# Layer 0's scaled blocks added by one VectorE reduce a tile, all form additions on GpSimd, form sets for all seven outer terms

## The chip, the core and the metric

The kernel runs on one core of a Trainium2 chip. TensorE (PE) multiplies matrices into PSUM; VectorE (DVE), ScalarE (ACT) and GpSimd (POOL) work on tiles in SBUF, and the first two also read PSUM; SyncE (SP) here only issues DMA transfers. Each engine takes its instructions in one stream, and a stream waits on counters (semaphores) that other engines and transfers raise. The metric is the device time in microseconds (us); lower is better. All numbers are float32.

## The reference

Input: x of shape (B=8, N=2048, F=64), a dense row-normalised adjacency A of 2048 x 2048, and small weights. Four layers follow each other, each `x = layernorm(x + layer(x))`:

```python
# layer 0: Chebyshev supports [I, A, 2 A A - I], weights made per node from an embedding with D = 16
w = einsum('nd,dkio->nkio', embedding, weight);  b = einsum('nd,do->no', embedding, bias)
out = einsum('bnki,nkio->bno', einsum('knm,bmc->bnkc', A_stack, x), w) + b
# layer 1: twice  z = relu((A @ z) @ W_i)
# layer 2: x @ W_self + (A @ x) @ W_neighbor + bias
# layer 3: concat(x, A x, 2 A A x - x, A x, 2 A A x - x) @ W + bias
```

What costs time is the product of the 2048 x 2048 matrix A with a 2048 x 512 block (all batches and features side by side), which is needed seven times, and layer 0's product with per-node weights: for each node the 64 features of three supports are multiplied with 16 matrices, and the 16 results are added with the node's 16 embedding values as factors.

## The kernel before

**Products with A.** The first product is made while A comes in, slice by slice, and on the way VectorE stores sums of blocks of A ("comb") in DRAM. The other six are calls of `product`, counted here as products one (layer 0's second) to six, each a fast scheme at two levels; four and six add their result in place. At the outer level A is taken as 2 x 2 blocks of 1024, and seven "outer terms" (A11, S1, A12, S2, S4, S3, A22 in order of time) are multiplied. Within a term there are two recipes:

- `inner`: a scheme of seven products of 512 x 512 blocks. `mul` loads 1 MB into a ring of buffers "a", seven of its eight chunks in all, and issues four matmuls of 512 columns (or 16 of 128 when the result is added in place into xy, `onto_slot`); the PSUM tiles are mma, mmb, mmc. A matmul in float32 shows as two records in the profile.
- `fast_inner`: 26 smaller products in 13 pairs (`PAIRS`), each with an operand from a "set of forms" of that term (26 blocks of 256 KB that lie in DRAM) and with one from x, made on GpSimd by seven additions of 512 values a partition and four of 256 (f, d, fn, fm). It has 52 matmuls of 256 columns, or 104 of 128 in place; the PSUM tiles are mm.

A set of forms is made once, by the generator `make_forms`, from four 1 MB tiles of the term: four raw blocks are stored as they are (`RAW`), and the list `SUMS` names 28 additions or subtractions of 128 x 512; 22 of the results are stored, one DMA each, issued by SP (L270). Those named in `POOLED` (ten) are GpSimd's, the other eighteen VectorE's (L290, L293). Four terms (`FORMED`) have sets: S1's is made in layer 0's product, those of A12, S2 and S4 at the start of the second.

**Layer 0's feature step.** `product(1, feature0)` hands each finished quarter block to `feature0(g, p, hT)`: 16 groups, each of four node tiles of 128 for one pair of batches. For each tile, TensorE multiplies the three supports (x, A x, A A x, as the tiles xT, tT and C) with the weights wn into two PSUM tiles y, eight matrices each (L1519; four y buffers). VectorE scales and adds the first eight blocks onto xy (L1529, one scalar_tensor_tensor each, with the node's embedding value as the factor); ScalarE scales the other eight into the SBUF tile s (L1533), and GpSimd adds those up in halves, 512, 256 and 128 values, and then onto xy (L1539, L1542). `fetch` (L1498) loads xT and tT of the next group through SP, into two buffers each.

**Order.** `Pump` runs the feature steps between terms. In layer 0 they are held back: four groups run after term S2, twelve at the start of the second product, and beside them the forms' generator is stepped (`Pump.run` with `side` and `rate`). After it the second product's seven terms follow. The instructions under `keep_in_program_order` stay in the order in which they are written on their engine; others are placed by a scheduler when the program is built. Each engine, SP too, then executes its own fixed order. SP's order holds the loads of A and of forms (L249, L252, L254), the stores of forms (L270) and the fetches (L1498).

## Time and profile before

| | us |
|---|---|
| median of 3 runs | 1649.23 (1647.22 to 1649.6) |
| profiled execution, its own time | 1647.88 |
| its span | 1646.0 |
| layer 0's feature step, first run (four groups) | from 306.6 |
| layer 0's feature step, second run (twelve groups) | 464.0 to 711.8 |
| second product's first matmul | 715.0 |

| engine | busy us | share of the span |
|---|---|---|
| TensorE, matmul | 1623.3 | 99% |
| TensorE, weight loads (beside the matmuls) | 1154.6 | 70% |
| VectorE | 1122.0 | 68% |
| ScalarE | 308.7 | 19% |
| GpSimd | 574.5 | 35% |

The profile shows one execution. For each group of instructions it gives how often it ran, its busy time and the mean of one; for idle time it names what ended it. The chain of work that ended last is followed back from the last instruction: what stands in it set the time. A name like `y<-wn,xT` is an output tile and its inputs; L1519 is line 1519 of the kernel.

### The profile page before, as it was taken

The numbers are of one execution on the slowest core, as the hardware profiler recorded it, in microseconds if no ns is written. First come the engines' busy times: TensorE is split into PE (matmuls) and PEld (weight loads), VectorE is DVE, ScalarE is ACT, GpSimd is POOL, SyncE is SP. The second block draws the span as 40 slices with busy tenths as digits, with TensorE's granted clock in tenths as the row PEclk, the third lists the DMA queues.
The fourth block names the chain that finished last, engine by engine and source line by source line (L and its number), as shares of the span: only waits on it lengthen the run. The fifth ranks groups of instructions, "written<-read, shape, count | busy, mean of one in ns | idle before, by whom it ended". The sixth has DMA issues, their size and how long they took to land.

```text
span 1646.0 us, 23252 instructions
## 1 busy us (share of the span) xinstructions
PE 1623.3 (99%) x8886; PEld 1154.6 (70%) x8886; DVE 1122.0 (68%) x1889; ACT 308.7 (19%) x870; POOL 574.5 (35%) x582
## 2 busy tenths in 40 slices
PE   9999999999999999999999999999999999999998
PEld 5998944444444444438865787589999788669998
DVE  5996885686458878846753477974688556644687
ACT  0210100143024444421111111221111112100111
POOL 1121100284037778764502350034512441025510
PEclk9999999999999999999999999999999999999999
DMA  8999999746853645278777776566888866677885
GB/s 315 358 389 370 334 342 326 250 141 237 307 178 123 203 141 187 101 310 312 277 287 262 288 280 253 208 227 234 295 293 301 292 234 213 237 255 282 310 307 175
DMA packets 101390, 429.47 MB, mean 261 GB/s; under 512 B 10752, under 2 KB 31616, under 8 KB 61856
## 3 DMA queue, kind: packets, MB, share of 16 engines
q1 hardware_dynamic: 87616, 380.34, 64.8%
q0 software_dynamic: 12016, 46.27, 7.5%
q8 instruction: 71, 1.16, 0.3%
q10 hardware_dynamic: 1648, 1.38, 0.3%
q14 instruction: 39, 0.32, 0.1%
HBM read 346.16 MB, written 81.79 MB: 260 GB/s over the span
## 4 chain that ended last, share of the span: by engine, by line
PE 94%; DVE 3%; DMA 1%; issue 1%; POOL 0%; ACT 0%; ACTq 0%; SPq 0%; DVEq 0%; POOLq 0%
PE y L1519 19%; PE mm L443 15%; PE mm L437 10%; PE mmb L565 10%; PE mmc L565 7%; PE mma L565 7%; PE ps_n L1301 6%; PE mmb L558 4%; PE ps_i L1215 3%; PE z L1573 3%; PE mmc L558 2%; PE mma L558 2%; PE z L1602 2%; PE ps_n L1255 1%; PE pt L1564 1%
## 5 line engine op out<-in xcount | busy, mean ns | idle before, releaser
L1539 POOL TENSOR_TENSOR s<-s 128x512 f32<-128x512 f32 (+2 forms) x192 | 166.2, 865 | 254.3 <-ACT s L1533 244.1
L1529 DVE SCALAR_TENSOR_TENSOR xy<-y,e_sb,xy 128x128 f32<-128x128 f32 x512 | 179.4, 350 | 65.3 <-PE y L1519 49.4
L1533 ACT ACTIVATE s<-y,e_sb 128x128 f32<-128x128 f32 x512 | 139.3, 383 | 196.2 <-PE y L1519 178.3
L565 PE MATMUL mmb<-a,t 128*128 128x512 f32 x360 | 161.9, 592 | 0.0
L443 PE MATMUL mm<-a,f 128*128 128x256 f32 x576 | 135.1, 380 | 1.1 <-POOL f L389 1.0
L1519 PE MATMUL y<-wn,xT 64*128 64x512 f32 x512 | 131.4, 590 | 0.0
L1519 PE MATMUL y<-wn,C 64*128 64x512 f32 x512 | 131.2, 589 | 0.0
L1519 PE MATMUL y<-wn,tT 64*128 64x512 f32 x512 | 131.1, 589 | 0.0
L389 POOL TENSOR_TENSOR f<-T 128x512 f32<-128x512 f32 x20 | 26.5, 1340 | 276.7 <-PE mmb L565 124.7
L565 PEld LDWEIGHTS mmb<-a,t 128*128 128x128 f32 x360 | 67.3, 190 | 79.4 <-issue 78.7
L443 PEld LDWEIGHTS mm<-a,f 128*128 128x128 f32 x576 | 108.7, 190 | 17.7 <-POOL f L389 1.9
L437 PE MATMUL mm<-f,a 128*128 128x128 f32 x768 | 92.4, 275 | 0.0
L1519 PEld LDWEIGHTS y<-wn,xT 64*128 64x128 f32 x512 | 49.5, 187 | 60.9 <-issue 57.3
L1519 PEld LDWEIGHTS y<-wn,tT 64*128 64x128 f32 x512 | 49.6, 187 | 60.2 <-issue 59.7
L1519 PEld LDWEIGHTS y<-wn,C 64*128 64x128 f32 x512 | 49.5, 187 | 60.4 <-issue 60.4
L437 PEld LDWEIGHTS mm<-f,a 128*128 128x128 f32 x768 | 89.0, 192 | 0.1
L476 DVE TENSOR_TENSOR p<-p,mm 128x512 f32<-128x512 f32 x60 | 41.0, 684 | 61.3 <-PE mm L443 41.7
L319 DVE TENSOR_TENSOR u<-mmb,p 128x512 f32<-128x512 f32 x44 | 30.2, 686 | 67.5 <-PE mmb L565 58.1
L466 DVE TENSOR_TENSOR C<-C,mm 128x512 f32<-128x512 f32 x80 | 54.2, 684 | 29.3 <-PE mm L443 22.3
L565 PE MATMUL mma<-a,T 128*128 128x512 f32 x160 | 72.1, 593 | 0.0
L1023 POOL DMA_DIRECT2D comb<-si x29 | 22.0, 758 | 137.8 <-DVE si L1014 137.8
L558 PE MATMUL mmb<-t,a 128*128 128x128 f32 x576 | 67.3, 275 | 0.0
(243 smaller groups left out, 3024.7 us busy)
## 6 DMA issues: line engine op xcount, KB each, us to landing
a<-comb SPq DMA_DIRECT2D x127, 1024.0 KB, 5.0
a<-form SPq DMA_DIRECT2D x120, 1024.0 KB, 4.8
a<-in_blocks SPq DMA_DIRECT2D x43, 1024.0 KB, 4.9
comb<-si POOLq DMA_DIRECT2D x29, 1024.0 KB, 10.6
form<-form SPq DMA_DIRECT2D x88, 256.0 KB, 2.8
a<-in_slices SPq DMA_DIRECT2D x15, 1024.0 KB, 10.9
comb<-so POOLq DMA_DIRECT2D x15, 1024.0 KB, 12.8
a<-form SPq DMA_DIRECT2D x20, 512.0 KB, 4.8
```

Of the source, the lines that this page charges most:

```text
L437: nc.tensor.matmul(ps[:, ts(2 * h + j, P)], a[:, j, m, :], x[:, m, :], start=(start and h == j == m == 0), stop=(m == 1), skip_group_check ...
L443: nc.tensor.matmul(ps[:, ts(h, GW // 2)], x[:, m, :], a[:, :, m, :], start=(start and h == m == 0), stop=(m == 1), skip_group_check=True,)
L466: nc.vector.tensor_tensor(out, out, view(v), op)
L558: nc.tensor.matmul(to, a[:, k, m, :], xb[:, m, :], start=(start and opens and m == 0), stop=(m == TG - 1), skip_group_check=True,)
L565: nc.tensor.matmul(ps, xb[:, m, :], a[:, :, m, :], start=(start and m == 0), stop=(m == TG - 1), skip_group_check=True,)
L1215: nc.tensor.matmul(ps, x[:, m // 2, m % 2], s[n](m), start=(start and m == 0), stop=(m == TG - 1), skip_group_check=True,)
L1301: nc.tensor.matmul(ps[:, ts(p, GW // 2)], b(k, p), a(k // TG, k % TG), start=(start and p == k == 0), stop=(k == NT // 2 - 1), skip_group_ ...
L1519: mm = nc.tensor.matmul(y[:, b, :], terms[n][half, ts(k, P)], wn[half, n, h * DH : (h + 1) * DH, :], start=(n == 0), stop=(n == 2),)
L1529: tc.keep_in_program_order(nc.vector.scalar_tensor_tensor(acc, y[:, :, ts(d, F)], e, acc, ALU.mult, ALU.add))
L1533: nc.scalar.activation(s[:, d], y[:, :, ts(d, F)], AF.Copy, scale=e)
L1539: nc.gpsimd.tensor_tensor(s[:, :n], s[:, :n], s[:, n : 2 * n], ALU.add)
L1573: nc.tensor.matmul(z[:, k, :], aT[:, ts(k, P)], wd[:, w, :], start=(n == 0), stop=(n == len(terms) - 1),)
```

## The change

Three things change together.

1. **Layer 0's tile.** VectorE's scalar_tensor_tensor now takes six of the sixteen blocks (`DIRECT = 6`), and the sixth writes its sum to slot 0 of a larger tile s. ScalarE scales the other ten into slots 1 to 10. One VectorE tensor_reduce adds the eleven slots into xy. It is issued by `settle` after the next tile's six additions, or when `Pump.run` ends. GpSimd has no part in it any more.
2. **The forms' additions.** All 28 additions of a set are GpSimd's; two negations a set ("n", "m"), by ScalarE, take the place of the three-operand form that VectorE had. `SUMS` is reordered. When a tile of a set has been read for the last time, the next set's tiles are loaded (`COMING`); the third and fourth tile lie in buffers "T" where several sets are made in a row.
3. **Seven sets instead of four.** Layer 0's product makes S3's set beside its first four groups and uses it. The second product makes six sets (S1, A12, S2, S4, A22, A11) beside its twelve groups, at 2.02 steps of the generator for each step of the features (1.08 before), and uses all but A11's itself. Products three to five form all seven terms; the last forms all but A22.

The descriptor scratch of the DMAs that GpSimd issues is halved (`dynamic_dma_scratch_size`).

```diff
@@ -22,7 +22,7 @@
 
 A11, A12, A22, S1, S2, S3, S4 = range(7)
 A21 = 7
-FORMED = (S1, A12, S2, S4)
+FORMED = (S1, A12, S2, S4, S3, A22, A11)
 
 
 
@@ -37,17 +37,17 @@
 ROWS = ((0, 0), (1, 0), (0, 1), (1, 1))
 RAW = {11: (2, 2), 14: (1, 1), 19: (0, 2), 23: (1, 0)}
 SUMS = (
-    (16, (0, 1), (0, 3), 1), (5, (2, 0), (2, 3), 1), ("d", (2, 1), (2, 2), 1), ("c", (0, 0), (0, 2), 1),
-    (6, 16, (1, 3), 0), (18, 6, "d", 1), (21, (1, 1), "d", 1), (4, 21, (1, 2), 1),
-    (1, (1, 3), (2, 3), 1), (2, 1, (2, 0), 1), (15, 2, "c", -1), (0, "c", (1, 0), 0),
-    (20, (1, 2), 0, -1), (10, (3, 1), (3, 2), 1), ("f", 10, (3, 3), 1), (17, "f", 1, -1),
-    (7, (0, 1), 10, -1), ("b", (0, 0), (1, 0), 1), (12, (0, 3), (1, 3), 1), (24, (3, 0), (3, 2), 1),
-    (3, (2, 0), 24, -1), ("a", (1, 1), (2, 1), 1), (8, (3, 0), (2, 0), -1), (22, (3, 1), (0, 1), -1),
-    (9, 7, "b", -1), ("e", 24, (3, 3), 1), (13, "e", 12, -1), (25, 3, "a", -1),
+    (5, (2, 0), (2, 3), 1), ("n", (0, 0), None, None), ("c", "n", (0, 2), -1), (0, "c", (1, 0), -1),
+    (20, (1, 2), 0, -1), (1, (1, 3), (2, 3), 1), (2, 1, (2, 0), 1), (15, 2, "c", 1), (10, (3, 1), (3, 2), 1),
+    ("f", 10, (3, 3), 1), (17, "f", 1, -1), (7, (0, 1), 10, -1), ("b", (0, 0), (1, 0), 1), (9, 7, "b", -1),
+    (16, (0, 1), (0, 3), 1), ("d", (2, 1), (2, 2), 1), ("m", (1, 3), None, None), (6, "m", 16, -1),
+    (18, 6, "d", 1), (21, (1, 1), "d", 1), (4, 21, (1, 2), 1), (24, (3, 0), (3, 2), 1), (3, (2, 0), 24, -1),
+    ("a", (1, 1), (2, 1), 1), (25, 3, "a", -1), (8, (3, 0), (2, 0), -1), (22, (3, 1), (0, 1), -1),
+    (12, (0, 3), (1, 3), 1), ("e", 24, (3, 3), 1), (13, "e", 12, -1),
 )
 HALF = {13: 0, 22: 0, 8: 1, 17: 1}
-POOLED = {5, 18, 4, 15, 20, 17, 12, 22, 9, 25}
-SPENT = 24
+COMING = (8, 12, 16, 26)
+DIRECT = 6
 
 
 def unit(i, j):
@@ -61,6 +61,7 @@
     def __init__(self):
         self.jobs = []
         self.later = []
+        self.ended = None
         self.rate = 1
         self.gate = None
         self.owed = 0
@@ -114,6 +115,8 @@
                         side.pop(0)
             self.jobs.pop(0)
             n = None if n is None else n - 1
+        if self.ended is not None:
+            self.ended()
         for job in side:
             for _ in job:
                 pass
@@ -171,7 +174,6 @@
     DH = D // 2
     RING = 4
     TB = 9
-    LANDING = 4
     BLK = TG * GW
 
     big = ctx.enter_context(tc.tile_pool(name="big", bufs=1))
@@ -237,12 +239,15 @@
     pieces = []
     p_mm = p_y = None
 
-    def load(q, s, forms=False):
+    def load(q, s, forms=False, home=None):
         nonlocal loads
-        loads += 1
-        turn = loads % (RING + 3)
-        pool = ring2 if ring2 is not None and turn >= RING else ring
-        a = pool.tile([P, TG, TG, P], F32, tag="a", name="a")
+        if home is None:
+            loads += 1
+            turn = loads % (RING + 3)
+            pool = ring2 if ring2 is not None and turn >= RING else ring
+            a = pool.tile([P, TG, TG, P], F32, tag="a", name="a")
+        else:
+            a = home
         flat = a.rearrange("p n m c -> p (n m c)")
         if forms:
             size = min(4, len(SLOT) - 4 * s) * GW
@@ -259,7 +264,7 @@
             tc.keep_in_program_order(pieces.pop(0)())
         return a
 
-    def make_forms(*qs):
+    def make_forms(*qs, landing):
 
 
         pin = tc.keep_in_program_order
@@ -269,8 +274,13 @@
             dst = formed[q][k // 4][:, ts(k % 4, GW)]
             nc.sync.dma_start(dst.rearrange("p (n m c) -> p n m c", n=2, m=2), f)
 
-        coming = [load(qs[0], s) for s in range(4)]
-        for _ in range(LANDING):
+        def fetch(q, s):
+            return load(q, s, home=None if len(qs) == 1 or s < 2 else sums.tile(
+                [P, NT // 2, 4 * F], F32, tag="T", name="T", bufs=3
+            ).rearrange("p t c -> p (t c)").rearrange("p (n m c) -> p n m c", n=TG, m=TG))
+
+        coming = [fetch(qs[0], s) for s in range(4)]
+        for _ in range(landing):
             yield
         for i, q in enumerate(qs):
             tiles, coming, made, done = coming, [], {}, []
@@ -286,23 +296,20 @@
                 store(q, n, raw(*ik))
             for k, (n, a, b, sign) in enumerate(SUMS):
                 f = sums.tile([P, 2, 2, P], F32, tag="t", name="form", bufs=TB)
-                if sign == 0:
-                    pin(nc.vector.scalar_tensor_tensor(f, source(a), -1.0, source(b), ALU.mult, ALU.subtract))
-                else:
-                    eng = nc.gpsimd if n in POOLED else nc.vector
-                    pin(eng.tensor_tensor(f, source(a), source(b), ALU.add if sign > 0 else ALU.subtract))
                 made[n] = f
+                if sign is None:
+                    nc.scalar.activation(f, source(a), AF.Copy, scale=-1.0)
+                    continue
+                pin(nc.gpsimd.tensor_tensor(f, source(a), source(b), ALU.add if sign > 0 else ALU.subtract))
                 if not isinstance(n, str):
-                    done.append((q, n, f))
+                    done.append((n, f))
                 yield
                 while len(done) > 1:
-                    store(*done.pop(0))
-                if k > SPENT and len(coming) < 2 and i + 1 < len(qs):
-                    coming.append(load(qs[i + 1], len(coming)))
+                    store(q, *done.pop(0))
+                while i + 1 < len(qs) and len(coming) < 4 and k >= COMING[len(coming)]:
+                    coming.append(fetch(qs[i + 1], len(coming)))
             for job in done:
-                store(*job)
-            while len(coming) < 4 and i + 1 < len(qs):
-                coming.append(load(qs[i + 1], len(coming)))
+                store(q, *job)
 
     def product(src, feature, between=None, rate=1, own=None, pin=False, runs=None, onto_slot=None, ends=False, fast=(), forms={}):
 
@@ -707,10 +714,10 @@
                 yield
 
         def side(q, b=None):
-            return [make_forms(*forms[q]), prepare_sums(b)] if q in forms else []
+            return [make_forms(*forms[q], landing=8 if waits else 5), prepare_sums(b)] if q in forms else []
 
         if waits:
-            pump.run(None, side(A11, b11), 1.08)
+            pump.run(None, side(A11, b11), 2.02)
             pump.hold = False
         pump.pass_mark()
 
@@ -1497,6 +1504,17 @@
                     for tile_, src in zip(fetched[i, p], (xT, t1T)):
                         pin(nc.sync.dma_start(tile_, src[p][:, ts(i, GW)]))
 
+            open_sums = []
+
+            def settle():
+                while open_sums:
+                    acc, s = open_sums.pop(0)
+                    tc.keep_in_program_order(
+                        nc.vector.tensor_reduce(acc, s.rearrange("p d b f -> p b f d"), AX.X, ALU.add)
+                    )
+
+            pump.ended = settle
+
             def feature0(g, p, hT):
                 if (g, p) == order[0]:
 
@@ -1510,7 +1528,7 @@
                     acc = xy[:, 0, t, ts(p, 2 * F)].rearrange("p (b f) -> p b f", f=F)
 
 
-                    s = l0y.tile([P, DH, 2, F], F32, tag="s", name="s", bufs=2)
+                    s = l0y.tile([P, D - DIRECT + 1, 2, F], F32, tag="s", name="s", bufs=2)
                     for h in range(2):
                         y = p_y.tile([P, 2, DH * F], F32, tag="y", name="y")
                         for n in range(3):
@@ -1525,26 +1543,23 @@
                                     tc.keep_in_program_order(mm)
                         for d in range(DH):
                             e = e_sb[:, t, h * DH + d : h * DH + d + 1]
-                            if h == 0:
+                            if h == 0 and d < DIRECT:
                                 tc.keep_in_program_order(nc.vector.scalar_tensor_tensor(
-                                    acc, y[:, :, ts(d, F)], e, acc, ALU.mult, ALU.add
+                                    s[:, 0] if d == DIRECT - 1 else acc, y[:, :, ts(d, F)], e, acc, ALU.mult, ALU.add
                                 ))
                             else:
-                                nc.scalar.activation(s[:, d], y[:, :, ts(d, F)], AF.Copy, scale=e)
+                                nc.scalar.activation(
+                                    s[:, 1 + h * DH + d - DIRECT], y[:, :, ts(d, F)], AF.Copy, scale=e
+                                )
                         if h == 0:
+                            settle()
                             yield
-                    n = DH // 2
-                    while n:
-                        tc.keep_in_program_order(
-                            nc.gpsimd.tensor_tensor(s[:, :n], s[:, :n], s[:, n : 2 * n], ALU.add)
-                        )
-                        n //= 2
-                    tc.keep_in_program_order(nc.gpsimd.tensor_tensor(acc, acc, s[:, 0], ALU.add))
+                    open_sums.append((acc, s))
                     yield
 
 
             RUNS = {A12: 1, S2: NP}
-            product(1, then(feature0, 0, gap=4), lambda: pump.add(sum_wn()), rate=4, runs=RUNS, forms={S2: (S1,)})
+            product(1, then(feature0, 0, gap=4), lambda: pump.add(sum_wn()), rate=4, runs=RUNS, forms={S2: (S3,)}, fast=(S3,))
 
 
     late = p_z = None
@@ -1586,7 +1601,7 @@
         nc.vector.scalar_tensor_tensor(part(g, p, 0), z, 0.0, part(g, p, 0), ALU.max, ALU.add)
         yield
 
-    product(0, feature1a, to_late, pin=True, fast=FORMED, forms={A11: (A12, S2, S4)})
+    product(0, feature1a, to_late, pin=True, fast=FORMED[:6], forms={A11: (S1, A12, S2, S4, A22, A11)})
     def both_terms(src, w, b):
 
         def own(g, p):
@@ -1659,7 +1674,7 @@
         ("w_l3", np.asarray(L3_gnn_weight)),
         ("b_l3", np.asarray(L3_gnn_bias).reshape(1, F)),
     ]
-    nc = bacc.Bacc("TRN2", target_bir_lowering=False, num_devices=1, dynamic_dma_scratch_size=8192)
+    nc = bacc.Bacc("TRN2", target_bir_lowering=False, num_devices=1, dynamic_dma_scratch_size=4096)
     arrays, args = {}, []
     for name, a in layout:
         a = np.ascontiguousarray(a)
```

## The prediction

> **What bounds the kernel now.** I read the page's busy table first, then the chain that ended last, then stages of it by window, and last the waits of the queues that the change touches. A "set" below is the forms of one outer term (28 GpSimd adds after the change); a "group" is one run of layer 0's feature step, four node tiles.
>
> ```profile
> span 1646.0 us, 23252 instructions
> PE 1623.3 (99%) x8886; PEld 1154.6 (70%) x8886; DVE 1122.0 (68%) x1889; ACT 308.7 (19%) x870; POOL 574.5 (35%) x582
> ...
> PE 94%; DVE 3%; DMA 1%; issue 1%; POOL 0%; ACT 0%; ACTq 0%; SPq 0%; DVEq 0%; POOLq 0%
> PE y L1519 19%; PE mm L443 15%; PE mm L437 10%; PE mmb L565 10%; PE mmc L565 7%; PE mma L565 7%; PE ps_n L1301 6%; PE mmb L558 4%; PE ps_i L1215 3%; PE z L1573 3%; PE mmc L558 2%; PE mma L558 2%; PE z L1602 2%; PE ps_n L1255 1%; PE pt L1564 1%
> ```
>
> TensorE is busy 99% of the span and is 94% of the chain; the next stretch of the chain is always another matmul. So only two things can move the time: fewer matmul columns, or a wait that TensorE does not have now.
>
> ```profile
> core 0: us, PE busy (x) PEld busy (x) DVE busy (x) ACT busy (x) POOL busy (x), PEclk, DMA share, GB/s
> ...
> 464.00:711.80 247.80, 247.42 (x1153) 111.44 (x1152) 195.70 (x467) 108.06 (x386) 187.05 (x218) 1.00 0.45 147
> ```
>
> This window is the second and longer stretch of layer 0's projection (the "main run": 12 groups, 48 tiles, the y matmuls). The columns are busy times by engine; TensorE has no gap: 247.8/48 = 5.16 us a tile, 20.6 a group. VectorE and GpSimd have room (196 and 187 of 248), so neither limits it.
>
> ```profile
> 464.02 239.70 PE y L1519 x1116
> 708.25 6.65 DMA a<-in_blocks
> 715.03 5.29 PE mma L565 x8
> ...
> 801.40 34.54 PE mm L443 x160
> ...
> 1483.62 3.57 PE mmc L558 x32
> ...
> 1494.34 69.69 PE mm L437 x624
> ```
>
> Start, length, work. Here are the prices of a term by both recipes: a plain inner product is 7 products of 3.43 us (3.57 when it adds in place), a formed one is 52 matmuls of 256 columns or 104 of 128. 160 records in 34.54 us are 0.216 each, and a formed term has 104 such records: 22.5 against 24.0 us. In place, 624 records in 69.69 us are three terms of 23.2 against 25.0. The 6.65 us of DMA at 708.25 is the one place where TensorE waited for a load.
>
> ```profile
> 673.82 0.38 SPq L1498 DMA_DIRECT2D xT<-in_xT  x1
> 674.30 0.40 SPq L1498 DMA_DIRECT2D tT<-t1T  x1
> 674.79 33.40 SPq L270 DMA_DIRECT2D form<-form  x11
> 708.25 0.42 SPq L252 DMA_DIRECT2D a<-in_blocks  x1
> ```
>
> This is SP's queue around that wait: 11 stores of forms, each held until its form is made, and behind them the first load of the next product, issued the moment the last store went. SP issues strictly in its order. What stands behind a store of a form waits for that form.
>
> ```profile
> L293 DVE TENSOR_TENSOR form<-a x36: 677/685/1759, 317.6 to 692.0; 128x512 f32<-128x512 f32 x36
> L293 POOL TENSOR_TENSOR form<-form x20: 1264/1276/1756, 332.9 to 706.6; 128x512 f32<-128x512 f32 x20
> ```
>
> ```profile
> 725.72 1.27 POOL L389 TENSOR_TENSOR d<-T 128x512 f32<-128x512 f32 x1
> 727.07 1.27 POOL L392 TENSOR_TENSOR f<-d,T 128x512 f32<-128x512 f32 x1
> 728.29 1.27 POOL L389 TENSOR_TENSOR f<-d,T 128x512 f32<-128x512 f32 x1
> ...
> 775.16 1.27 POOL L389 TENSOR_TENSOR fn<-xy,f 128x512 f32<-128x512 f32 x1
> 776.39 1.27 POOL L392 TENSOR_TENSOR fm<-f,xy 128x512 f32<-128x512 f32 x1
> ```
>
> Min/median/max in ns: the same 128x512 add takes 0.685 us on VectorE and 1.27 on GpSimd. Back to back on GpSimd, starts are 1.22 to 1.23 us apart, and 1.35 where an add needs the one just before it (d, then f<-d).
>
> **The change, part by part.**
>
> *Formed terms (removes matmul columns).* 20 terms are formed now, 34 after. New in the first product: S3; in the second: S3, A22; in products three to five: A11, S3, A22 each; in the last: A11, S3. Nine are not in place, five are (products four and six): 9 x 1.54 + 5 x 1.78 = 22.8 us less, all on the path. Their GpSimd operands (seven adds of 1.23 and four half ones of about 0.7, some 12 us a term against 22.5 of TensorE) fit, also back to back; their loads shrink from 7 MB to 6.5. I take -23, ends -23 and -17 (a short wait at some boundaries).
>
> *The tile's sum.* VectorE loses 2 of 8 scalar_tensor_tensor (0.351 each) a tile and gains one reduce of 11x128 values. The existing reduces take 1.21 us for 1024 values and 2.28 for 2048, so 1.6 for 1408; its 512-byte stride is shown by no row, so up to twice, 3.2. VectorE then has 2.1 + 1.6 = 3.7 us a tile (5.3 at worst), ScalarE ten scaled copies at 0.272 busy each = 2.7, both under TensorE's 5.16. Cost nothing; at the worst end 0.15 us on some 30 tiles, +5. The reduce stands behind the next tile's six adds, so it does not wait for ScalarE. GpSimd loses its four adds a tile, about 3 us.
>
> *Six sets on GpSimd in the main run.* This is the part that decides. Before, 18 of a set's 28 adds were VectorE's, pinned between the tiles' own VectorE work, so forms kept TensorE's pace: 7 to 11 stores stand on SP between two fetches of xT/tT (the next group's operands). After, all 168 adds (6 x 28) are a stream of GpSimd's own, and the built order of the changed program puts far more of them ahead of each fetch. Counting GpSimd's adds of the main run that precede each fetch on SP:
>
> ```
> fetch for group   6    7    8    9    10   (11 to 15 follow directly)
> adds ahead       35   69  102  137   168
> ```
>
> ScalarE is bound the same way: the two negations of a set ("n", "m") stand in its order between the scaled copies. The last, m of set A11, comes after 322 of 640 copies, two copies into group 8, and waits for a buffer whose last reader is the set's tenth add, number 150.
>
> TensorE would want group 6 at 41 us into the run and group 10 at 124. GpSimd's first add can start when set S1's first two tiles land, about 1.5 us before the run (their ring buffers come free 10.3 and 6.9 us before it, and such loads land in 5.0). Twelve adds of a set need the one just before, 16 do not: (12 x 1.36 + 16 x 1.23)/28 = 1.29 us apart. The forms in the present run average 1.42 where they meet VectorE's adds; most of those are gone, and VectorE idles while TensorE waits, so I take 1.32, between the uncontended row and the contended one (1.43 apart) and nearer the first. Add 150 ends at -1.5 + 150 x 1.32 = 196.5, m at 197. TensorE by then has filled the four y buffers, 2.5 tiles into group 8. ScalarE's eight copies free the first, 3 us; then 29.5 tiles x 5.16 = 152; and 1.8 us for the slow restart (in the chain, 8 records after the DMA wait took 5.29 instead of 3.43). The run ends at 354. The fetch of group 10 gives nearly the same: -1.5 + 168 x 1.32 + about 1 to issue + 4.9 to land + 6 x 20.6 = 350. Today the next product starts 251.0 us after the run began, 252.7 with its slow restart. Its loads now go out while the last groups run, so that wait is gone within the 354. Together +101; ends with the spacing at 1.23 and 1.43: +88 and +118. Tile loads that come late (budget 7.9 us between the freeing add and the first use, 5.0 needed now, 10.9 in the row of in_slices, a busier stage) would add up to 3.8 on five sets, +19; the stage would move some 66 MB in 220 us, 300 GB/s, at which loads of forms land in 4.8 elsewhere, so I take 0.
>
> *One set (S3) in the first projection run (four groups).* All 28 adds stand ahead of group 2's fetch. Their fourth tile lands 5 us into the run, then 25 x 1.32: 38.5, four more loads and the fetch to issue 2.5, landing 4.9: 46, wanted at 41. +5; ends 0 and +10.
>
> *Formed S3 before plain A22 in layer 0.* VectorE first ends S3's joins and last four adds (0.69 each, some 4.6 us with the last join), then A22's first two sums (1.4), wanted 3.4 us after A22 starts: +3; ends 0 and +6.
>
> *Smaller scratch for GpSimd-issued DMAs.* 44 stores of 1 MB in the first 200 us, 4.5 apart, landing in 10.6 to 12.8: two to three in flight. No issue waits now (0.76 us each). 0, unless fewer than three fit; two would cost 44 x 5.3 - 200 = +33 or more. Counted under the slow rival.
>
> Sum: -23 + 101 + 5 + 3 = +86. The profiled execution took 1647.9 (span 1646.0), 1.3 under the median of 1649.2; 0.2% (3.3 us) is what this kernel's runs can tell apart. Forecast: 1649 + 86 = 1735.
>
> **Two rules of the Trainium skill.** "GPSIMD Engine Reference", section "4.1 Engine selection", speaks against the change: it sends elementwise adds on a tile to VectorE, GpSimd being about twice as slow with two inputs. The rows above say 1.27 against 0.685, 1.86 times. Twice 0.685 would be 1.37 an add and the time 1742 by an estimate from that page.
>
> "SBUF — State Buffer", section "Who interferes with whom", speaks for it: a VectorE instruction with two SBUF inputs blocks a GpSimd one that reads SBUF, a tensor_reduce never does on trn2. The form rows' tails to 1.76 on both engines agree, as does the scalar_tensor_tensor on PSUM at 337 to 352 ns with no tail. By that rule the spacing would be near 1.29, 4.5 us less, 1731 by the same estimate.
>
> **Rivals.** *A, the forecast: GpSimd's stream holds SP's fetches and ScalarE's copies, and TensorE waits about 100 us in the main run: 1735, its own range 1710 to 1765; 75%.*
>
> *B, the other side: GpSimd keeps up.* Then only the savings stay: 1649 - 23 - 5.4 (the load wait and restart at 708) + 3 = 1624. It decides where the run's loss is under 15 us: -1.5 + 150p + 157.5 = 267.7, p = 0.745 us an add. Against it: no GpSimd add of this shape took under 1.26. For it: only a wait read wrongly out of the built order. 8%.
>
> *C, same side, dearer:* spacing of 1.43 and late tiles, or a scratch for two stores: +16 to +36 more, 1751 to 1771; 15%.
>
> *D, the stalls are half:* if TensorE gets further ahead before the last hold than the four y buffers allow by my count, or GpSimd starts earlier, some 1690; 2%. That the change isn't in the program can be left out: all 168 adds stand on GpSimd.
>
> **From these the numbers.** Slower: A, C and D, 92%, nearly all far beyond 0.2%; faster: B, 7%; same: 1%. The range leaves out B, D and the end of C: 1705 to 1775; it takes in both spacings (-13, +17), the late tiles (+19) and the first run's ends.
>
> **What would show it.** In the profile after: GpSimd busy nearly without a gap for some 220 us from the start of the main run; TensorE idle there about 100 us, in pieces of several us, ended by y buffers that ScalarE's copies free, with ScalarE waiting for GpSimd's forms; the y run about 350 long instead of 248; its last seven to eight groups at 20.6 each without a gap; no load wait at the next product. A reduce near 1.6 us, formed terms at 22.5 and 23.2. The prediction is wrong if GpSimd's adds come at under a microsecond, if fetches pass the stores, or if the formed terms wait for their GpSimd operands.

## The result and the profile after

The changed kernel takes **1780.06 us** (median of 4 runs, 1779.7 to 1781.41) against 1648.34 for the kernel before on the same chip: a ratio of **1.08, interval 1.0782 to 1.0819**. That is slower, as forecast, but by 132 us and not by 86, and it lies 5 us above the range. The profiled execution has a span of 1778.0 us, 132.0 more than before.

The stages of the two spans, and what the forecast gave to each (all in us). "Between" are the three outer terms between the two runs of the feature step; a run is counted to the next matmul that is not its own:

| stage | before | after | difference | forecast |
|---|---|---|---|---|
| up to the first run | 306.55 | 306.79 | +0.2 | 0 |
| first run (four groups) | 82.60 | 98.91 | +16.3 | +5 |
| between | 74.80 | 75.05 | +0.3 | +1.5 |
| main run (twelve groups) | 251.08 | 359.71 | +108.6 | +101 |
| rest (the next product's first matmul to the end) | 930.97 | 937.54 | +6.6 | -21.5 |
| sum | 1646.0 | 1778.0 | +132.0 | +86 |

First the page of the changed kernel: the span, the busy shares, and the chain that ended last by engine.

```profile
span 1778.0 us, 24390 instructions
PE 1638.5 (92%) x9238; PEld 1241.5 (70%) x9238; DVE 1237.2 (70%) x1823; ACT 359.3 (20%) x1036; POOL 772.8 (43%) x642
...
PE 61%; DVE 21%; POOL 8%; DMA 5%; issue 2%; ACT 1%; POOLq 0%; SPq 0%; ACTq 0%; DVEq 0%
```

TensorE is busy for 1638.5 us, 15 more than before although it does less work (in the windows below, where it waits often, its granted clock is 0.77 to 0.79, and the same columns take longer). It is idle for 8% of the span, where it was idle for 1%. In the chain its share falls from 94% to 61%; VectorE, GpSimd and the DMAs have taken 34%.

Next the windows: two in the middle of the main run, and one after GpSimd's stream had ended. The columns are busy times by engine, then the granted TensorE clock, the DMA share and GB/s.

```profile
core 0: us, PE busy (x) PEld busy (x) DVE busy (x) ACT busy (x) POOL busy (x), PEclk, DMA share, GB/s
520.00:580.00 60.00, 31.86 (x120) 13.26 (x120) 23.20 (x35) 14.81 (x53) 57.96 (x47) 0.77 0.98 326
580.00:640.00 60.00, 34.94 (x124) 14.60 (x126) 23.33 (x35) 18.65 (x65) 57.81 (x48) 0.79 0.93 315
700.00:760.00 60.00, 59.41 (x278) 26.91 (x280) 56.49 (x89) 33.41 (x122) 0.00 (x0) 1.00 0.13 37
```

GpSimd is busy 58 of 60 us, TensorE 32 to 35 of 60, and the granted clock is at 0.77 to 0.79. Once GpSimd has nothing left to do (0.00), TensorE is at 59.4 of 60 and the clock at 1.00.

Then the chain, at the end of the hold, and ScalarE's timeline there.

```profile
658.95 2.33 POOL form L303
665.29 2.50 POOL form L303 x2
667.80 4.04 DMA form<-form
678.20 8.11 PE y L1537 x24
```

```profile
662.47 0.63 ACT L1551 ACTIVATE s<-y,e_sb 128x128 f32<-128x128 f32 x2 [6.31 <-DVE s L1547]
674.51 0.63 ACT L301 ACTIVATE form<-T 128x512 f32<-128x512 f32 x1 [11.41 <-POOL form L303]
675.04 1.04 ACT L888 ACTIVATE sq<-xy 128x1024 f32<-128x1024 f32 x1
675.99 4.74 ACT L1551 ACTIVATE s<-y,e_sb 128x128 f32<-128x128 f32 x18
```

Up to 674.5 the chain is GpSimd's additions and, between them, stores of forms and loads of their tiles, as at 667.80. The 0.63 us of L301 at 674.51 are "m" of set A11: it came 11.41 us after ScalarE's previous instruction, released by a GpSimd form. Behind it stand ScalarE's copies (L1551), behind them the y buffers, and TensorE resumes at 678.20. What waited in the main run, engine, releaser, total, times, longest:

```profile
PEld y L1537 <- ACT s L1551: 99.8, 25, 13.7
...
ACT form L301 <- POOL form L303: 98.2, 7, 16.7
PE y L1537 <- ACT s L1551: 85.0, 15, 12.9
```

ScalarE's negations wait 98 us for GpSimd's forms in seven places, and TensorE's matmuls wait for ScalarE's copies in fifteen. GpSimd itself does not wait: between its first and last add of the run (479.18 to 698.73, 168 adds) there is no gap over 0.6 us.

### The profile page after: what moved, and what is told of

It reads as the page before. It is cut to its first block, busy times and chain, and to the rows that moved or that the text cites. A ratio compares the mean times of both kernels' runs of the same rounds, so it can differ in the third digit from the quotient of the medians.

```text
span 1778.0 us, 24390 instructions
## 1 busy us (share of the span) xinstructions
PE 1638.5 (92%) x9238; PEld 1241.5 (70%) x9238; DVE 1237.2 (70%) x1823; ACT 359.3 (20%) x1036; POOL 772.8 (43%) x642
## 4 chain that ended last, share of the span: by engine, by line
PE 61%; DVE 21%; POOL 8%; DMA 5%; issue 2%; ACT 1%; POOLq 0%; SPq 0%; ACTq 0%; DVEq 0%
PE mm L450 22%; PE mm L444 16%; POOL form L303 8%; PE ps_n L1308 5%; DVE xy L1513 5%; PE mmb L572 4%; PE y L1537 3%; DVE xy L1547 3%; PE mmc L572 3%; PE mma L572 2%; PE z L1588 2%; PE ps_i L1222 2%; PE z L1617 2%; DMA form<-form 1%; DVE ss L895 1%
## 5 line engine op out<-in xcount | busy, mean ns | idle before, releaser
L1513 DVE TENSOR_REDUCE xy<-s 128x128 f32<-128x1408 f32 x64 | 167.0, 2609 | 105.3 <-ACT s L1551 105.3
L450 PE MATMUL mm<-a,f 128*128 128x256 f32 x1008 | 238.0, 381 | 1.1 <-POOL f L396 1.0
L450 PEld LDWEIGHTS mm<-a,f 128*128 128x128 f32 x1008 | 190.7, 191 | 28.3 <-POOL f L396 1.9
L1551 ACT ACTIVATE s<-y,e_sb 128x128 f32<-128x128 f32 x640 | 171.7, 403 | 121.1 <-DVE s L1547 116.3
L444 PE MATMUL mm<-f,a 128*128 128x128 f32 x1248 | 153.6, 278 | 5.5 <-DVE u L492 5.5
L444 PEld LDWEIGHTS mm<-f,a 128*128 128x128 f32 x1248 | 147.9, 195 | 5.8 <-DVE u L492 5.7
L473 DVE TENSOR_TENSOR C<-C,mm 128x512 f32<-128x512 f32 x145 | 98.3, 683 | 65.0 <-PE mm L450 50.2
L1547 DVE SCALAR_TENSOR_TENSOR xy<-y,e_sb,xy 128x128 f32<-128x128 f32 x320 | 111.9, 350 | 35.3 <-PE y L1537 25.9
L450 PE MATMUL mm<-a,T 128*128 128x256 f32 x416 | 100.8, 380 | 0.0
L396 POOL TENSOR_TENSOR f<-xy 128x512 f32<-128x512 f32 x28 | 38.5, 1388 | 118.4 <-PE mm L450 63.6
L450 PEld LDWEIGHTS mm<-a,T 128*128 128x128 f32 x416 | 77.3, 190 | 10.2
```

The source lines that it names most:

```text
L396: nc.gpsimd.tensor_tensor(out, a, c, ALU.subtract)
L444: nc.tensor.matmul(ps[:, ts(2 * h + j, P)], a[:, j, m, :], x[:, m, :], start=(start and h == j == m == 0), stop=(m == 1), skip_group_check ...
L450: nc.tensor.matmul(ps[:, ts(h, GW // 2)], x[:, m, :], a[:, :, m, :], start=(start and h == m == 0), stop=(m == 1), skip_group_check=True,)
L473: nc.vector.tensor_tensor(out, out, view(v), op)
L1513: nc.vector.tensor_reduce(acc, s.rearrange("p d b f -> p b f d"), AX.X, ALU.add)
L1547: tc.keep_in_program_order(nc.vector.scalar_tensor_tensor(s[:, 0] if d == DIRECT - 1 else acc, y[:, :, ts(d, F)], e, acc, ALU.mult, ALU.add))
```

## The experiments

**One: the tile's sum alone.** The kernel before with VectorE's six direct blocks, ScalarE's ten and the reduce; forms, their engines and their number as before. The halved scratch is in it too.

```diff
-                            if h == 0:
+                            if h == 0 and d < DIRECT:
...
-                    n = DH // 2
-                    while n:
...
+                    open_sums.append((acc, s))
```

> The kernel before with the new tile sum alone (six VectorE adds and one reduce, ten ScalarE copies, GpSimd's four adds gone); the forms stay three sets in the second run, on both engines. Theory: the reduce took 2.6 us in the changed kernel, so a tile costs VectorE 6 x 0.351 + 2.6 = 4.7 us, and beside the form additions (18 of 28 a set, 0.69 to 0.99 us each, 37 to 53 us in the second run) and the norms (some 30 us) VectorE needs about 300 us for a run of 248: the second run becomes some 290 to 310 us long and the total 1648 + 45 to 70. Rival: the sum is hidden behind TensorE also here, total within 5 us of before.

Measured: 1686.03 against 1649.59, ratio 1.0224 (1.0207 to 1.0241), +36.4; the main run is 281.7 long (+30.6), the first 86.8 (+4.2). The tile sum is not free, so "within 5 us" falls; it is cheaper than the 45 to 70 us expected. The run by windows:

```profile
530.00:590.00 60.00, 53.84 (x242) 23.58 (x240) 57.03 (x93) 28.19 (x100) 6.37 (x5) 0.97 0.53 171
590.00:650.00 60.00, 55.38 (x250) 23.14 (x248) 57.60 (x89) 30.60 (x111) 11.39 (x9) 1.00 0.48 149
```

VectorE, the third pair of numbers, is busy 57 of 60 and has become the limit; TensorE has 54 to 55. VectorE still has 18 of a set's 28 additions here, which the changed kernel gives to GpSimd, so this price doesn't simply add to the others.

**Two: the same instructions in the order of the code.** The changed kernel, with stores, tile loads, fetches, negations and ScalarE's copies pinned to the order in which they are written. It removes nothing.

```diff
-            nc.sync.dma_start(dst.rearrange("p (n m c) -> p n m c", n=2, m=2), f)
+            pin(nc.sync.dma_start(dst.rearrange("p (n m c) -> p n m c", n=2, m=2), f))
...
-                    nc.scalar.activation(f, source(a), AF.Copy, scale=-1.0)
+                    pin(nc.scalar.activation(f, source(a), AF.Copy, scale=-1.0))
...
-                    fetch(order.index((g, p)) + 1)
+                    fetch(order.index((g, p)) + 1, tc.keep_in_program_order)
```

> The changed kernel with the same instructions, but the stores of forms, the loads of their tiles, the fetches, the negations and ScalarE's scaled copies keep the order in which they are written: 15 to 17 additions instead of 31 to 35 stand ahead of each fetch of the second run, and the last negation comes after group 14.8 instead of 8.05. Theory (TensorE is held by the order, not by the amount of GpSimd's work): the second run falls from 366 to 250 to 265 us, bound by TensorE (248) or VectorE (48 x 4.7 + 30 = 256), the first run's 9.5 us wait goes too, total 1780 - 110 = 1670 (1660 to 1680). Rival (GpSimd's additions or the transfers, 98% busy in that run, are the limit in themselves): the run stays above 330 us, total over 1740.

Measured: 1675.73, ratio 1.0162 (1.0147 to 1.0177), 104 us less than the changed kernel with the same adds on the same engine. The first run is back at 82.6; the main run, at 271.5, stays 6 us over the 250 to 265 expected. So it is the place of the fetches and negations behind GpSimd's stream that costs, not the length of that stream. Counted in the built program as in the prediction's table, the adds of the main run ahead of the fetches for groups 6 to 15 are now 5, 20, 36, 51, 64, 80, 97, 112, 125 and 140; in the changed kernel they are 35, 69, 102, 137 and then 168 for all that follow. The 20 us that remain over the kernel before have two visible parts. One is at the end, in the chain:

```profile
724.14 3.72 POOL form L303 x3
727.94 1.28 POOL form L303
729.65 6.81 DMA a<-in_blocks
736.59 5.19 PE mma L572 x8
```

The stream now ends last, and the next product's first load stands behind its last stores: TensorE waits 9.8 us. The other is VectorE, 55 and 57 busy of 60 in two windows of the run, as in experiment one.

**Three: is ScalarE's hold or SP's the one that counts?** The negations go to GpSimd, which frees ScalarE of every wait for a form; SP's order stays.

```diff
-                    nc.scalar.activation(f, source(a), AF.Copy, scale=-1.0)
+                    nc.gpsimd.tensor_scalar(f, source(a), -1.0, None, ALU.mult)
```

> The changed kernel with the two negations of a set on GpSimd (tensor_scalar) instead of ScalarE, nothing else: ScalarE's order then holds no instruction that waits for a form, while SP's fetches still stand behind GpSimd's stream (the fetch of group 10 behind all 180 operations of the main run, 168 adds and 12 negations). In the changed kernel every idle piece of TensorE in the main run was ended by ScalarE's copies. If SP's hold is enough by itself: 180 x 1.3 - 1.5 + 6 to issue and land + 6 x 20.6 = 362, the main run stays at 350-375 (359.7) and the idle pieces are ended by loads of xT or tT. If ScalarE's negations alone held it, the main run falls to 290 or less.

Measured: 1794.54 in one run, the main run 371.1. TensorE's waits in it, and the tile xT's loads:

```profile
PE y L1537 <- DMA xT<-in_xT: 107.4, 5, 28.3
...
PE y L1537 <- ACT s L1551: 1.5, 2, 1.1
```

Five waits of 14 to 28 us, 107.4 in all, now ended by loads of xT; ScalarE's copies end 1.5 us. So there are two holds in the same place, about equally long: take ScalarE's away and SP's shows. The trace of the changed kernel names only ScalarE, and who trusted that line alone would have mended the wrong queue. (The 12 more operations of 1.49 us make GpSimd's stream 18 us longer, and the run got longer by 11.) The other half, SP's order mended and ScalarE's kept, was not run; that ScalarE's hold is as long by itself is read from the changed kernel's trace alone.

**Four: the rest without the operand adds.** This kernel leaves the eleven GpSimd additions on x of each formed term out and feeds raw columns instead.

```diff
-            less(f4, two(xb(1, 0)), xp(2, 0))
...
-            plus(fm, f2, xp(2, 1))
...
+            raw = [xb(k, j) for k in range(4) for j in range(2)]
+            forms = {n: raw[n % 8] for n in range(26)}
```

> The changed kernel without the eleven GpSimd additions that make the x operands of a formed term: raw blocks of x are multiplied in their place, so the results are not the reference's; all else runs. After layer 0 GpSimd then has next to nothing to do. Theory (its additions slow VectorE's additions that read two SBUF tiles, and TensorE then waits for VectorE): VectorE's 128x512 additions there come back to 0.68 us, the waits that VectorE ends go from some 27 us to under 8, and the stretch from the second product's first matmul to the end falls from 937.5 to about 912 (931 before, less 21 for the 13 formed terms). Rival (a formed term simply has more VectorE work): VectorE's waits stay and the stretch is still about 935.

Measured: 1752.81 in one run, the rest 912.1 instead of 937.5. The rest of the changed kernel and of this one, as windows:

```profile
core 0: us, PE busy (x) PEld busy (x) DVE busy (x) ACT busy (x) POOL busy (x), PEclk, DMA share, GB/s
840.46:1778.00 937.54, 905.52 (x6088) 824.88 (x6088) 658.35 (x968) 135.96 (x275) 476.49 (x382) 0.99 0.72 258
```

```profile
838.96:1751.00 912.04, 897.81 (x6088) 821.23 (x6088) 612.21 (x968) 135.85 (x275) 39.75 (x18) 0.99 0.74 265
```

VectorE has the same 968 instructions in both and is busy 658 us in the one and 612 in the other: its adds are 46 us longer where GpSimd adds too. GpSimd's suffer as well: over all formed terms of the changed kernel, the groups of its 512-value operand adds have means of 1.28 to 1.49 us, against 1.27 alone. One group of VectorE's, the additions of a partial sum u onto the result C, both in SBUF, shows it best, in the changed kernel and without the operand adds (min, median and max in ns):

```profile
L473 DVE TENSOR_TENSOR C<-C,u x58: 640/737/1796, 449.9 to 1742.2; 128x512 f32<-128x512 f32 x58
```

```profile
L454 DVE TENSOR_TENSOR C<-C,u x58: 647/691/694, 451.2 to 1715.4; 128x512 f32<-128x512 f32 x58
```

0.69 us alone, up to 1.80 beside GpSimd. The 145 additions of the same size with one operand in PSUM (C<-C,mm) stay at 0.69 at most in both. This is what "Who interferes with whom" in "SBUF — State Buffer" of the Trainium skill states: a VectorE instruction with two SBUF inputs and a GpSimd instruction that reads SBUF exclude each other, and the one issued first goes first. The prediction used that rule only where it spoke for the change. In the rest it speaks against it, and the trace agrees. TensorE feels it inside the terms and at their ends. Its largest waits for VectorE in the rest, changed kernel and then without the operand adds (total, times, longest):

```profile
PE mm L450 <- DVE u L483: 6.7, 4, 2.2
PE mm L444 <- DVE u L492: 5.5, 1, 5.5
PE mm L444 <- DVE u L483: 3.9, 1, 3.9
PE z L1588 <- DVE C L326: 3.4, 1, 3.4
```

```profile
PE mm L425 <- DVE u L473: 4.0, 1, 4.0
PE mm L425 <- DVE xy L451: 1.2, 1, 1.2
PE mm L425 <- DVE u L464: 0.6, 1, 0.6
```

The wait of 3.9 us, with VectorE's and GpSimd's work before it:

```profile
1244.66 2.07 PE L444 MATMUL mm<-fn,a 128*128 128x128 f32 x8 [3.92 <-DVE u L483]
```

```profile
1237.18 2.29 DVE L477 TENSOR_TENSOR C<-C,p 128x1024 f32<-128x1024 f32 x1
1239.40 2.81 DVE L792 TENSOR_TENSOR T<-xy 128x2048 f32<-128x2048 f32 x1
```

```profile
1236.36 2.03 POOL L396 TENSOR_TENSOR f<-d,T 128x512 f32<-128x512 f32 x1 [0.45 <-PE mm L444]
1238.36 4.44 POOL L399 TENSOR_TENSOR f<-T,f 128x256 f32<-128x256 f32 x2
```

Without the operand adds the same two VectorE instructions take 1.22 and 2.29 us, and TensorE waits 0.63 at this place. The longest wait, 5.5 us, is another case: there VectorE meets GpSimd's two additions that close a quarter (L744, in the kernel before too), and without the operand adds it is still 4.0. TensorE's waits of over 0.6 us in the rest, those within it, sum to 22.8 us, and to 5.8 without the operand adds. Its 6088 records are also busy 7.7 us longer (905.5 against 897.8): the eight before the wait above take 1.06 us, the eight behind it 2.07. Together that is nearly all of the 25.4.

**Five: only the old four formed terms in products two to six.** Everything else of the changed kernel stays, the sets too.

```diff
-    product(0, feature1a, to_late, pin=True, fast=FORMED[:6], forms={A11: (S1, A12, S2, S4, A22, A11)})
+    product(0, feature1a, to_late, pin=True, fast=FORMED[:4], forms={A11: (S1, A12, S2, S4, A22, A11)})
...
-    product(0, then(nothing, 1), onto_slot=1, fast=FORMED)
+    product(0, then(nothing, 1), onto_slot=1, fast=FORMED[:4])
```

> The changed kernel in which products two to six form only the four terms that were formed before (S1, A12, S2, S4); all the sets are still made. Theory (the nine newly formed kinds of terms there cost more in waits than the 21 us of matmuls they save): the stretch after layer 0 takes 928 to 934 us instead of 937.5, layer 0's runs are unchanged, total some 4 to 9 us less than the changed kernel. Rival (the new terms do save, and the loss lies elsewhere): total 10 to 20 us more than the changed kernel.

Measured: 1774.66 in one run; the rest 931.5, within 1 us of the kernel before (930.97). So the thirteen newly formed terms save nothing there: they cost 6 us more (937.5) than leaving them plain.

**Six: is it the reduce's stride?** Program order as in experiment two, with the scaled blocks laid out so that the eleven values of one sum lie side by side.

```diff
-                        nc.vector.tensor_reduce(acc, s.rearrange("p d b f -> p b f d"), AX.X, ALU.add)
+                        nc.vector.tensor_reduce(acc, s, AX.X, ALU.add)
...
-                    s = l0y.tile([P, D - DIRECT + 1, 2, F], F32, tag="s", name="s", bufs=2)
+                    s = l0y.tile([P, 2, F, D - DIRECT + 1], F32, tag="s", name="s", bufs=2)
```

> The kernel with program order, and the scaled blocks laid out so that the reduce reads its eleven values side by side: s is [128, 2, 64, 11] instead of [128, 11, 2, 64]; ScalarE's copies and the sixth scalar_tensor_tensor then write at a stride of 44 bytes. If the 512-byte stride of its input made the reduce dear (2.60 us against 1.6 by the contiguous rows of before), it takes 1.6 to 1.75 here, VectorE falls from 4.7 to about 3.8 a tile, under TensorE's 5.16, and the second run falls from 271.5 to 250-263 us (total 1655-1668). Rival: the number of values sets its price, it stays at 2.6 and the second run within 4 us of 271.5. Second rival: ScalarE's strided writes get dearer (0.272 a copy now); at over 0.5 its ten copies outlast TensorE's tile and the second run is longer than 271.5.

The reduce in the changed kernel, and with the new layout (min, median, max in ns):

```profile
L1513 DVE TENSOR_REDUCE xy<-s x64: 2547/2604/2645, 317.0 to 845.7; 128x128 f32<-128x1408 f32 x64
```

```profile
L1513 DVE TENSOR_REDUCE xy<-s x64: 1593/1597/1620, 317.4 to 724.5; 128x128 f32<-128x1408 f32 x64
```

The estimate of 1.6 us holds for contiguous values; the 512-byte stride costs 1.0 us more. ScalarE's copies, which write at a stride now, go from a median of 393 to 496 ns each, and ScalarE is busy 33 to 35 of 60 us in the windows of the run. The time falls to 1666.03, ratio 1.0102 (1.0087 to 1.0117). The main run is 265.0, a little over the range of 250 to 263: VectorE is out of the way (42 to 51 of 60 in the windows), but GpSimd's stream still ends last, and the next product's load still waits 10.4 us for its stores.

**Seven and eight: the operand adds on VectorE**, once in the kernel with program order, once in the kernel before.

```diff
-                nc.gpsimd.tensor_tensor(out, a, c, ALU.subtract)
+                nc.vector.tensor_tensor(out, a, c, ALU.subtract)
...
-                nc.gpsimd.tensor_tensor(out, a, c, ALU.add)
+                nc.vector.tensor_tensor(out, a, c, ALU.add)
```

> The kernel with program order, with the eleven x operand adds of a formed term on VectorE instead of GpSimd. Without those adds the rest (from the next product's first matmul to the end) fell from 937.5 to 912.1. If what costs there is the meeting of GpSimd's adds with VectorE's, it is gone here too: VectorE's adds return to 0.69, the added ones take 7 x 0.69 + 4 x 0.35 = 6.2 us a term beside 22.5 of TensorE, and the rest is 912-922 (936.7 with program order alone). Rival: VectorE lacks the time or the place in its order at the terms' ends, and the rest stays at 930 or more.

> The kernel before with its x operand adds on VectorE instead of GpSimd, nothing else. TensorE lost 16.7 us of the rest (930.9) beyond its steady pitch, part of it behind VectorE's adds. If the same contention is in the kernel before, the rest falls by 5 to 14 us (total 1635-1644); rival: with 20 formed terms there is little of it and VectorE's extra 6 us a term cost as much as they save, total within 3 us of 1649 or above.

Measured: 1664.83 in one run, the rest 926.8 (936.7 with program order alone): 10 us of the 25 come back, less than the 15 to 25 expected. VectorE's adds of the group shown in experiment four are at a median of 686 ns and at most 694 again, so the contention with the operand adds is gone, but VectorE now has 789 us to do in the rest and keeps TensorE waiting in its own right. In the kernel before the same step does nothing that can be told from no change: 1649.89 against 1649.32, ratio 1.0007 (0.9998 to 1.0017), the rest 931.6. The expected gain of 5 to 14 us is missed. With 20 formed terms, plain ones between them, neither price shows in the time; with 34 both do.

**Nine: program order, the contiguous reduce and the operand adds on VectorE together.**

> Program order, the contiguous reduce and the operand adds on VectorE together; six sets and 34 formed terms as in the changed kernel. If the three causes (queue order, reduce's stride, contention of operand adds) are separate and add: 306.5 to the first run, 82.6, 76, 250-263, 912-922 = 1627-1650 of span, 1629-1652 in all, that is about the kernel before or up to 1% under it. If the causes overlap, 1655 or more.

Measured: 1654.92, ratio 1.0035 (1.0022 to 1.0048); main run 265.3, rest 926.2. The total is 3 us over the range, since the main run and the rest end 2 and 4 us above theirs, and it lies at the 1655 named for causes that overlap. By the differences the two parts do add: in spans, the contiguous reduce takes off 8.5 us without and 9.4 with the operand adds on VectorE, these 10.5 and 11.4. SP's timeline at the end of the main run:

```profile
690.13 29.91 SPq L275 DMA_DIRECT2D form<-form  x19
720.13 0.38 SPq L257 DMA_DIRECT2D a<-in_blocks  x1
```

19 stores, each waiting for its form, and only then the next product's load.

**Ten and eleven: a shorter stream.** The last kernel with five sets in the main run (A11 stays plain later), and with six sets of which four adds each go to VectorE.

```diff
-    product(0, feature1a, to_late, pin=True, fast=FORMED[:6], forms={A11: (S1, A12, S2, S4, A22, A11)})
+    product(0, feature1a, to_late, pin=True, fast=FORMED[:6], forms={A11: (S1, A12, S2, S4, A22)})
...
-            pump.run(None, side(A11, b11), 2.02)
+            pump.run(None, side(A11, b11), 1.75)
```

```diff
+VECTOR = {12, 16, "a", "d"}
...
-                pin(nc.gpsimd.tensor_tensor(f, source(a), source(b), ALU.add if sign > 0 else ALU.subtract))
+                eng = nc.vector if n in VECTOR else nc.gpsimd
+                pin(eng.tensor_tensor(f, source(a), source(b), ALU.add if sign > 0 else ALU.subtract))
```

> The last combination (program order, contiguous reduce, operand adds on VectorE) without A11's set: the main run makes five sets (140 adds) at 1.75 steps of the generator for each step of the features, and products three to six leave A11 plain. In the last combination GpSimd's 168 adds ran from 482 to 719.7 and the next product's first load stood behind their last stores: TensorE waited 10.5 us at the end of the main run (265.3 long, 251.1 before). If GpSimd's length is what sets that wait, it is gone: main run 250-257; the rest loses four formed terms (4 x 1.5 to 1.8) and keeps 926-934; total 1641-1652. Rival: the wait stays, because the stores are held by something else than GpSimd's adds; main run 262 or more and total 1655-1663.

> The last combination with four of each set's 28 adds (12, 16, a, d) on VectorE, pinned between its tile work, six sets kept: GpSimd's adds in the main run fall from 168 to 144, about 31 us less; VectorE gains 24 x 0.69 = 17 us in a run in which it is busy some 205 of 265. If GpSimd's length sets the wait of 10.5 us at the run's end, the main run falls to 251-257 and the total to 1639-1648, under the kernel before (span 306.5 + 82.6 + 73 + 254 + 926 = 1642). Rival: VectorE's adds wait for GpSimd's or for tiles and hold its own tile work; main run 262 or more.

Measured: five sets 1649.33 against 1649.12, ratio 1.0 (0.9991 to 1.0009), main run 259.2, rest 924.8. Four adds on VectorE 1650.85, ratio 1.0014 (1.0005 to 1.0023), main run 260.3, rest 926.7. The wait at the run's end shrinks from 10.5 to 3.4 us (now ended by ScalarE's copies and not by a load) and to 6.4: the main runs lie between the two expectations. The first total is in its range, the second 3 us above, and neither kernel beats the one before. The whole loss of 132 us is accounted for and can be taken back in steps (spans): 1778.0, with program order 1673.3, with the contiguous reduce 1664.8, with the operand adds off GpSimd 1653.4, with five sets 1646.1 (the last step by making and using one set less). What is left of the change then is a rest 6 us shorter than before and a main run 8 us longer.

## Why the prediction was right, and where it failed

The direction, the place and the mechanism of the largest term were right; the total was 46 us short, and the measured time lies above the range.

- **The main run: right, +108.6 against +101.** GpSimd's first add came 1.57 us before the run (forecast 1.5), its adds 1.302 us apart over the 150 up to the one "m" waits for (1.32), "m" 193.8 us into the run (197), TensorE 3.7 us later (3). The last 29.5 tiles took 159.1 instead of 153.8, where VectorE, with the strided reduce at 4.70 a tile, is busy 152 of 162 us; and the next product waited 3.1 us more for ScalarE's copies, after which it restarted as slowly as before, where the forecast had that gone. That late tiles cost nothing was right: GpSimd had no gap. The spacing is near the 1.29 that followed from the rule on which VectorE instructions block GpSimd.
- **The -23 for the formed terms, taken because "their GpSimd operands" "fit, also back to back": this step failed, and it is the largest part, 28 us.** The rest got 6.6 us longer where 21.5 less were forecast. The saving itself was right: TensorE's records of a formed term are 0.216 and 0.112 us apart as before, so the 13 terms newly formed in the rest save 12.5 + 9.0 = 21.5 us. The operands did fit, too: TensorE waits for one of GpSimd's just once, 1.0 us. But the prediction compared only GpSimd's own time (12 us a term against 22.5), let waits at boundaries cost 6 us at most, and put what GpSimd's adds do to VectorE's at nothing. Experiments four and five show the price: 25.4 us for the operand adds, without which the rest comes within 3 us of the forecast, and a rest that is better off with the old four terms.
- **The first run: +16.3 against +5, outside the ends of 0 and 10.** The 28 adds ended 40.7 us in (38.5; the forecast's own terms, 5 + 25 x 1.32, give 38.0), since the fourth tile took 8.1 us to land and not 5. The fetch went out at 44.5 (41). Then it took 11.13 us to land instead of 4.9: four 1 MB tile loads had been issued in the 3 us before it, and the DMA share was at 0.99. TensorE waited 9.5 us and lost 1.9 in the slow restart, which the sum had left out here. SP's queue there, and the chain's pieces:

```profile
348.24 2.91 SPq L259 DMA_DIRECT2D a<-comb  x4
351.24 0.58 SPq L1505 DMA_DIRECT2D xT<-in_xT  x1
```

```profile
325.49 25.75 PE y L1537 x111
351.24 11.13 DMA xT<-in_xT
362.51 25.25 PE y L1537 x108
```

- **The tile's sum: 1.6 us forecast, 2.60 measured, the stride's price inside the stated bound of 3.2.** The +5 of that bound came, as part of the main run's 159.1.
- **S3 before A22: +3 forecast, 2.3 seen**, as one wait in A22; the stage grew by 0.3 where 1.5 was forecast, since an earlier wait shrank from 2.2 to 1.4. **The smaller scratch: 0, and 0.2 seen** up to the first run.
- **Rivals.** B asked for an add under 0.745 us; none was under 1.26. D's shorter hold did not come. C, at 1751 to 1771, came nearest in size, but by causes that did not occur: the spacing stayed at 1.302, no tile was late, the scratch was enough.

## What to carry to other kernels

When work moves to another engine, ask of each in-order queue what now stands behind it: here 104 of 132 us lay in where fetches and scaled copies stood, and the same adds in the order of the code took that back. Where one engine's trace line names the hold, look for a second queue with the same hold before mending one. An engine's idle time is not free for two-input adds if another engine adds from the same memory at the same time: the price appears in the other's busy time (here 658 us against 612), where the sum of one's own durations can't see it.

## What was not expected of the hardware

- A tensor_reduce over eleven values 512 bytes apart takes 2.60 us for 1408 values, 1.60 with the values side by side. Strided writes cost ScalarE 0.10 us for each copy of 128 values.
- A negation of 512 values a partition on GpSimd takes 1.49 us, more than an addition of two such tiles (1.27).
- 0.25 MB loads behind four 1 MB loads landed in 11.1 us at a DMA share of 0.99 (404 GB/s), and in 3.0 and 3.5 in the two other fetches of that run.
- TensorE's granted clock was 0.77 to 0.79 in the windows where it waited every few microseconds, so the work between the waits took longer too: the matmuls up to 678.20 were busy for 115.9 us, and the 18.5 tiles they make take 95.5 at 5.16.
